# A state-space layer and an attention layer on one core: image 0's norm loaded and computed first, weight transforms behind it, one activation table for Ln and Exp

## The chip, the cores and the metric

The kernel runs on one core of a Trainium2 chip. The metric is device time in microseconds of one execution. Three runs of the kernel before took 3,012.99, 3,017.89 and 3,022.72 us; their median is 3,017.89 us.

A core has five engines that each take their instructions in order: TensorE (PE in the profile, with PEld for its weight loads), VectorE (DVE), ScalarE (ACT), GpSimd (POOL) and SyncE (SP), which here only issues transfers. They meet through semaphores. A DMA, too, is issued by one of the engines and counts up a semaphore when it lands. An engine whose next instruction waits holds everything that stands behind it, whether or not that could run.

## What is computed

The input x holds four images of 512 channels and 32 x 32 points, all in float32. Layer 0 is a selective state-space layer over the 1,024 points of an image, layer 1 attention between convolutions. Both have a group norm ahead of them and the input added behind them.

```python
# layer 0, features = _gn(x), one sequence of 1024 points per image
xn = (x - mu) / jnp.sqrt(var + 1e-05) * ln_w + ln_b
xz = xn @ W_in
xm, z = (xz[..., :d_inner], xz[..., d_inner:])       # d_inner = 1024
xs = silu(causal_conv4(xm) + conv_b)
proj = xs @ W_x
dt = jax.nn.softplus(proj[..., :dt_rank] @ W_dt + b_dt)
Bm, Cm = ...                                         # 16 states each
# for each point
dA = jnp.exp(dt_t[..., None] * A)
h = dA * h + (dt_t * x_t)[..., None] * B_t[:, None, :]
y = jnp.einsum('bds,bs->bd', h, C_t)
out = ((y + xs * D_param) * silu(z)) @ W_out
# layer 1, on _gn(x)
x_bottom = conv3x3(x, w_bottom); sp_map = softmax(center @ top)
out = conv3x3(x + sp_map @ x_bottom, w_out)
```

`_gn` is a norm over groups of 16 channels and all points.

## The kernel before

**Layer 0** (to about 1,975 us) handles four images. Of an image it makes the norm, eight channel blocks of 128 (`xs`, by `conv1`, or for image 0 by `conv1_half` in two halves of 512 points), the gates (`gates`), the small projections (`params`), and then for each pair of channel blocks e and each half h a stage of 16 units, one for each state. `delta` begins a stage: dt by a matmul, a bias and softplus on ACT, dt times x (`dtx`, L793) on POOL, its transposes on PE and their copies (`dtxt`) on ACT. A unit (`unit`) makes a decay by Exp on ACT, the input term on ACT and PE or on POOL, a scan on DVE, a product with C on POOL (or for four states on DVE), and adds into PSUM by PE. While one image's units run, the next image's norm and projections are worked in between.

**Order.** The instructions are not issued in the order of the code. Every helper calls `step(engine, time, fn, reads, writes, prio, ...)`, and `Plan.issue` then lays the steps out: at each turn it takes, for each engine, the steps that could begin soonest by its own estimates and of these the one with the lowest `prio`. A step can name an activation table ("ln", "exp", "silu", "softplus"); if it isn't the one that the plan has loaded last, the step counts as late and costs `LOAD`. Steps with `fill=True` may come early or late. Buffers come from rings with a fixed number of slots.

**Image 0's norm** (`norms`, called with prio -60) loads x in four chunks of 512 KB on SP (L409), takes statistics on DVE (L425, L426), averages over groups by two small matmuls (L433, L449) with `deviation` (L261 to L265) between them, takes Ln (L458) and Exp (L463) for the root, and builds weights `mw` for the mean over channels. Then for both halves of the points: mean by matmuls (`pmu`, L394), L518 on DVE, squares on ACT (L532, into the two buffers "res"), their mean by matmuls (`pvar`, L539), Ln of both halves (L550), Exp of both (L556), L565 on DVE and the affine step on ACT (L575). `conv1_half` follows with the weights `winc` (L598, ring of two), matmuls `pxm` (L394), a first tap on ACT (L671), three on DVE (L682) and Silu (L695).

**Weight pieces** (`transform`) turn the 3x3 weights of layer 1 into their transformed form: 18 of 32 pieces are made in layer 0, the rest in layer 1 on DVE. A piece loads three tiles of 192 KB on SP (L1164), scales on ACT (L1169, L1170), does twelve operations on POOL (L1177 to L1197) and writes twelve stores on SP (L1204). The first `t0` = 11 have prio -190, the others 60 units apart:

```python
transform(u, src, k % NPC, -190 if k < PRM['t0'] else PRM['tg'] * (k - PRM['t0']))
```

**Small loads.** The two bias rows `brow_b` and `brow_o` and the small constants (`lnw_sb`, `lnb_sb`, ..., `a_sb`, `wx_sb`) are loaded on ACT's queue. `a_sb` goes through Exp on ACT (L309) and a product with -1 on DVE (L310). All transfers of SP and ACT share eight completion semaphores, taken in turn as they are laid out, so an issue may have to wait for an earlier transfer that holds the same one.

**The border of the layers.** `first_image` norms image 0 of layer 1's input at the end of layer 0: `root` takes Ln (L255) and Exp (L256). The other three images do this in layer 1 (`norm`).

Of the kernel before, what the change touches and what calls it, by code (L numbers as in the profile page):

```python
# [27 lines left out]
GS = 16  # L28


PRM = dict(pg=0.53, kt=2, ke=1, ka=-0.68, fl=0, fi=4.6, m0=45.7, n0=50.77, nl=2.05, q0=65.56, qg=5.2, c0=61.67, cg=6.03, p0=112, e0=3.46, eg=4.75, g0=78.98, gg=9.04, o0=13.03, og=5.23, dl=10.28, t0=11, tg=60)


class Buf:
# [21 lines left out]
class Plan:  # L56
# [7 lines left out]
    def __init__(self, slots, in_order):  # L64
        self.slots, self.steps = dict(slots), []
        self.queues = {r: [] for r in in_order}

    def buf(self, ring, make):
# [35 lines left out]
    def issue(self):  # L104
        ready = {e: [s for s in self.steps if s.eng == e and not s.unmet] for e in self.ENGINES}
        clock = {e: 0.0 for e in self.ENGINES}
        free = {r: [0.0] * n for r, n in self.slots.items()}
        queues = {r: list(q) for r, q in self.queues.items()}
        table, dma, left = None, 0.0, len(self.steps)
        waiting = sorted((s for s in self.steps if not s.fill), key=lambda s: -s.prio)  # L110
        while left:
            while waiting and waiting[-1].done is not None:
                waiting.pop()
            last = waiting[-1].prio + self.AHEAD if waiting else 1e9
            best = None
            for e in self.ENGINES:
                urgent = min((s.prio for s in ready[e] if s.table in (None, table)), default=1e9)
                found = []
                for s in ready[e]:
                    if s.prio > last:  # L120
                        continue
                    t = max(clock[e], s.ready)
                    for b in s.takes:
                        turn = b.free or b.ring not in queues or queues[b.ring][0] is b
                        t = max(t, min(free[b.ring])) if free[b.ring] and turn else 1e9
                    if t >= 1e9:
                        continue
# [12 lines left out]
            for b in s.takes:  # L140
                free[b.ring].remove(min(free[b.ring]))
                if b.ring in queues and not b.free:
                    queues[b.ring].pop(0)
            s.fn()
            if late:
                t += self.LOAD
                table = s.table
            clock[s.eng] = t + s.us
            s.done = clock[s.eng] + self.LAG[s.eng]
            if s.kb:  # L150
                dma = max(dma, s.done) + s.kb / 300
                s.done = dma + 2.0
            for b in s.bufs:
                b.left -= 1
                if b.ring and not b.left:
                    free[b.ring].append(s.done + self.HOP)
                    if b.done:
                        b.done(b.tile)
            ready[s.eng].remove(s)
            for u in s.users:  # L160
                u.unmet -= 1
                other = u.eng != s.eng or s.kb
                u.ready = max(u.ready, s.done + self.HOP if other else clock[s.eng])
                if not u.unmet:
                    ready[u.eng].append(u)
            left -= 1
# [3 lines left out]
def mamba_then_pab_kernel(  # L170
# [29 lines left out]
    spool = ctx.enter_context(tc.tile_pool(name="spool", bufs=2))  # L200
    dram = ctx.enter_context(tc.tile_pool(name="dram", bufs=1, space=DRAM))

    gm_sb = cpool.tile([P, P], F32, tag="gmat", name="gm_sb")
    nc.sync.dma_start(gm_sb, gmat)
    ident = cpool.tile([P, P], F32, tag="ident", name="ident")
# [68 lines left out]
    with ExitStack() as l0:  # L274
# [4 lines left out]
        yp = l0.enter_context(tc.tile_pool(name="l0y", bufs=1, space=PSUM))  # L279
        up = l0.enter_context(tc.tile_pool(name="l0u", bufs=4, space=PSUM))  # L280

        NT = L // P
        NK = T // P
        QC = C // 4
# [47 lines left out]
        def dram_set(name, shape, n=B):  # L332
# [11 lines left out]
        }  # L344
        plan = Plan(
            {**slots, "mm": 2, "u": 4, "y0": 1, "y1": 1},
            ("xt", "u", "h", "cbc", "bb", "dbx", "sc"),
        )
        step = plan.step
        MM, TR = 0.88, 0.114  # L350
# [50 lines left out]
        def norms(b, prio, lag=0.0):  # L401

            t = xts[b] = buf("xt", [P, NCC, L], f"xt_{b}")
            src = x[b].rearrange("(c p) h w -> p c (h w)", p=P)
            xin = [buf(None, None, "") for c in range(NCC)]
            step("SP", 0.0, lambda: t(), [], [], prio, holds=[t])
            for c in range(NCC):
                step(
                    "SP", 0.3, lambda c=c: nc.sync.dma_start(t()[:, c, :], src[:, c, :]),  # L409
                    [], [xin[c]], prio, kb=512, holds=[t],  # L410
                )
            spl = {}
# [26 lines left out]
            def mid():  # L439
# [16 lines left out]
            step(  # L456
                "ACT", 0.2,
                lambda: nc.scalar.activation(spl["dev"], pv()[:, :NCC], AF.Ln, bias=eps),  # L458
                [pv], [stat], prio, "ln",
            )  # L460
            step(
                "ACT", 0.2,
# [37 lines left out]
            )  # L500
            by_half = [buf(None, None, "") for h in range(NH)]
            by_chunk = by_token(NCC)
            for h, hs in enumerate(halves):
                prio += lag
                pmu = group(f"pmu_{b}_{h}",
                    [
                        (
# [2 lines left out]
                        )  # L510
                        for c in range(NCC)
                    ],
                    prio, holds=[t],
                )
                for c in range(NCC):
                    step(
# [5 lines left out]
                        [pmu], [by_half[h]], prio, holds=[t],  # L522
                    )
            pvars = []
            for h, hs in enumerate(halves):
                prio += lag
                pvar = buf("mm", [P, T], f"pvar_{b}_{h}")
                for c in range(NCC):
                    sq = buf("res", [P, T], f"sq_{b}_{h}_{c}")
                    step(  # L530
                        "ACT", 0.61,
                        lambda c=c, hs=hs, sq=sq: nc.scalar.activation(  # L532
                            sq(), t()[:, c, hs], AF.Square, bias=spl["nb"][:, c : c + 1]
                        ),
                        [by_half[h], stat], [sq], prio, holds=[t],
                    )
                    step(
                        "PE", MM,
                        lambda c=c, sq=sq, pvar=pvar: nc.tensor.matmul(  # L539
                            pvar(), mean_w, sq(), start=(c == 0), stop=(c == NCC - 1)  # L540
                        ),
                        [sq], [pvar], prio,
                    )
                pvars.append(pvar)

            rs = [buf("res", [P, T], f"rs_{b}_{h}") for h in range(NH)]
            for r, pvar in zip(rs, pvars):
                step(
                    "ACT", 0.58,
                    lambda r=r, pvar=pvar: nc.scalar.activation(r(), pvar(), AF.Ln, bias=eps),  # L550
                    [pvar], [r], prio, "ln",
                )
            for r, pvar in zip(rs, pvars):
                step(
                    "ACT", 0.52,
                    lambda r=r, pvar=pvar: nc.scalar.activation(pvar(), r(), AF.Exp, scale=-0.5),  # L556
                    [r], [pvar], prio, "exp",
                )
            prio += lag

# [25 lines left out]
                    affine(c, slice(0, L), by_chunk[c])  # L586
            else:
                for h, hs in enumerate(halves):
                    prio += 0.01
                    for c in range(NCC):  # L590
                        scaled(c, h)
                        affine(c, hs, [by_chunk[c][h]])
# [174 lines left out]
        def delta(b, e, h, prio):  # L767
# [20 lines left out]
            dtx = buf("dtx", [P, 2, T], f"dtx_{name}")  # L788
            us = [xs[b, 2 * e + j] for j in range(2)]

            def times():
                for j in range(2):
                    nc.gpsimd.tensor_mul(dtx()[:, j], dt()[:, j], us[j]()[:, hs])  # L793

            step(
                "POOL", 2.46, times, [dt, *(xh[b, 2 * e + j][h] for j in range(2))], [dtx], prio,
                holds=us,
            )
            dtxt = buf("dtxt", [P, NK, 2, P], f"dtxt_{name}")
# [275 lines left out]
        def first_image(prio):  # L1075
# [61 lines left out]
                spl["rstd"] = spool.tile([P, NCC], F32, tag="grstd", name="grstd_image")  # L1137
                rsqrt(spl["rstd"], pv()[:, :NCC])

            step("ACT", 1.7, root, [pv], [stat], prio, "ln")  # L1140
            for c in range(NCC):
                step(
                    "DVE", 0.76,
# [567 lines left out]
```

## Time and profile before

| what | us |
|---|---|
| median of three runs (range) | 3,017.89 (3,012.99 to 3,022.72) |
| the profiled execution | 3,013.52 |
| its span, first to last instruction | 3,011.5 |
| busy: PE, DVE, ACT, POOL | 2,732.6, 2,324.8, 1,846.0, 2,054.5 |
| granted TensorE clock, mean | 0.972 |
| POOL's first product with C, stage e0 h0 of image 0 | 132.86 |
| the same of stage e0 h1 of image 0 | 237.75 |
| the same of stage e0 h0 of images 1, 2, 3 | 641.02, 1,104.72, 1,582.70 |

A page of the profile tells of one execution. A line of the timeline has the start, the length, the engine, the line of the kernel, the operation, output and inputs and a count; in brackets the time that the engine stood idle before it, and what ended it. A group has busy time and the mean time of one instruction in ns. The share of a stretch that an engine is busy says what sets the pace there, and the stretches of this kernel differ.

### The profile page before, as it was taken

The numbers are of one execution on the slowest core, as the hardware profiler recorded it, in microseconds if no ns is written. First come the engines' busy times: TensorE is split into PE (matmuls) and PEld (weight loads), VectorE is DVE, ScalarE is ACT, GpSimd is POOL, SyncE is SP. The second block draws the span as 40 slices with busy tenths as digits, with TensorE's granted clock in tenths as the row PEclk, the third lists the DMA queues.
The fourth block names the chain that finished last, engine by engine and source line by source line (L and its number), as shares of the span: only waits on it lengthen the run. The fifth ranks groups of instructions, "written<-read, shape, count | busy, mean of one in ns | idle before, by whom it ended". The sixth has DMA issues, their size and how long they took to land.

```text
span 3011.5 us, 35733 instructions
## 1 busy us (share of the span) xinstructions
PE 2732.6 (91%) x11512; PEld 1611.4 (54%) x11512; DVE 2324.8 (77%) x2787; ACT 1846.0 (61%) x3186; POOL 2054.5 (68%) x1239
## 2 busy tenths in 40 slices
PE   4789789999889999879899988889999999999998
PEld 2346566656666566656666666544444444444444
DVE  3468999989999889899888999986968565346264
ACT  4569999999799998789999898731210013021000
POOL 7999987899977799977799999942241442314122
PEclk9899999999999999989999999999999999999999
DMA  6765644577734467834557754648789896627497
GB/s 175 221 195 165 198 135 145 162 217 231 233 117 151 151 198 226 254 111 140 153 168 218 224 173 149 161 150 303 213 303 283 300 332 243 245 86 263 142 320 256
DMA packets 408945, 610.46 MB, mean 203 GB/s; under 512 B 46488, under 2 KB 245400, under 8 KB 384184
## 3 DMA queue, kind: packets, MB, share of 16 engines
q1 hardware_dynamic: 399952, 593.67, 62.0%
q10 hardware_dynamic: 8648, 14.26, 1.3%
q8 instruction: 92, 1.51, 0.2%
q14 instruction: 93, 0.76, 0.1%
q0 software_dynamic: 160, 0.26, 0.0%
HBM read 511.09 MB, written 96.99 MB: 202 GB/s over the span
## 4 chain that ended last, share of the span: by engine, by line
PE 39%; ACT 14%; DVE 14%; POOL 6%; issue 5%; DMA 4%; SPq 0%; DVEq 0%; POOLq 0%; ACTq 0%
PE m_o L1501 11%; PE m_b L1501 8%; PE pat L1553 4%; PE y L917 4%; ACT sc L844 3%; DVE da L884 3%; PE po L394 3%; POOL da L907 3%; PE pz L394 2%; ACT da L832 2%; ACT u L832 2%; PE u L870 2%; DVE u L884 2%; DVE dbx L884 2%; PE pp L730 1%
## 5 line engine op out<-in xcount | busy, mean ns | idle before, releaser
L907 POOL TENSOR_TENSOR da<-da,cbc 128x1024 f32<-128x1024 f32 x288 | 681.2, 2368 | 83.3 <-DVE da L884 58.3
L859 POOL TENSOR_TENSOR dbx<-dtx,bbc 128x1024 f32<-128x1024 f32 x224 | 529.5, 2371 | 35.7 <-PE y L917 18.7
L844 ACT ACTIVATE sc<-dtxt,bt_sb 128x256 f32<-128x256 f32 x1152 | 506.8, 497 | 48.6 <-PE u L870 48.1
L832 ACT ACTIVATE da<-dt,a_sb 128x512 f32<-128x512 f32 x576 | 398.6, 712 | 41.2 <-PE y L917 27.0
L917 PE MATMUL y<-ident,da 128*128 128x128 f32 x2304 | 318.4, 282 | 65.3 <-POOL da L907 59.4
L884 DVE TENSOR_TENSOR_SCAN da<-da,carry_sb,u 128x512 f32<-128x512 f32 x288 | 355.8, 1262 | 25.7 <-PE u L870 20.2
L870 PE MATMUL u<-ident,sc 128*128 128x128 f32 x2304 | 329.3, 279 | 35.1 <-DVE da L884 26.6
L917 PEld LDWEIGHTS y<-ident,da 128*128 128x128 f32 x2304 | 267.4, 145 | 166.1 <-POOL da L907 124.7
L884 DVE TENSOR_TENSOR_SCAN da<-da,u 128x512 f32<-128x512 f32 x288 | 338.4, 1202 | 18.6 <-PE u L870 16.7
L1501 PE MATMUL m_o<-uw_o,v_o 128*128 128x512 f32 x768 | 335.6, 596 | 7.4 <-DMA uw_o<-u_o 7.4
L1501 PE MATMUL m_b<-uw_b,v_b 128*128 128x512 f32 x768 | 333.7, 593 | 5.0 <-ACT e_b L1509 2.5
L870 PEld LDWEIGHTS u<-ident,sc 128*128 128x128 f32 x2304 | 268.5, 143 | 111.3 <-issue 36.4
L832 ACT ACTIVATE u<-dt,a_sb 128x512 f32<-128x512 f32 x448 | 296.0, 679 | 21.0 <-DVE dbx L884 7.4
L917 PE MATMUL y<-ident,dbx 128*128 128x128 f32 x1792 | 254.0, 282 | 29.3 <-POOL dbx L907 20.1
L394 PE MATMUL pxm<-xt,winc 128*128 128x345 f32 (+3 forms) x704 | 249.2, 498 | 27.6 <-DMA winc<-in_w_in_dram 17.1
L917 PEld LDWEIGHTS y<-ident,dbx 128*128 128x128 f32 x1792 | 212.5, 145 | 97.8 <-POOL dbx L907 36.9
L394 PE MATMUL pz<-xt,winc 128*128 128x512 f32 x512 | 243.2, 602 | 8.9 <-issue 3.1
L1501 PEld LDWEIGHTS m_b<-uw_b,v_b 128*128 128x128 f32 x768 | 144.9, 190 | 190.1 <-issue 180.8
L1501 PEld LDWEIGHTS m_o<-uw_o,v_o 128*128 128x128 f32 x768 | 144.8, 191 | 189.9 <-issue 177.3
L907 POOL TENSOR_TENSOR dbx<-dbx,cbc 128x1024 f32<-128x1024 f32 x96 | 227.1, 2365 | 7.1 <-DVE dbx L884 2.5
L1553 PE MATMUL pat<-y_b,st 128*128 128x512 f32 x512 | 223.3, 597 | 1.6 <-DVE rz L1562 1.5
L394 PEld LDWEIGHTS pxm<-xt,winc 128*128 128x128 f32 x704 | 132.1, 198 | 115.8 <-issue 43.5
(235 smaller groups left out, 4288.8 us busy)
## 6 DMA issues: line engine op xcount, KB each, us to landing
cbc<-bcd SPq DMA_DIRECT2D x512, 256.0 KB, 3.6
uw_b<-u_b SPq DMA_DIRECT2D x96, 1024.0 KB, 4.8
uw_o<-u_o SPq DMA_DIRECT2D x96, 1024.0 KB, 4.8
bbc<-bcd SPq DMA_DIRECT2D x224, 256.0 KB, 3.6
u_b<-work SPq DMA_DIRECT2D x192, 128.0 KB, 2.9
winc<-in_w_in_dram SPq DMA_DIRECT2D x72, 256.0 KB, 3.6
szd<-sz SPq DMA_DIRECT2D x32, 512.0 KB, 3.6
szl<-szd SPq DMA_DIRECT2D x32, 512.0 KB, 4.9
```

Source lines behind the costliest of these rows:

```text
L394: lambda k=k, lhs=lhs, rhs=rhs: nc.tensor.matmul(p()[:, at : at + cols], lhs(), rhs(), start=(k == 0), stop=(k == n - 1)),
L730: lambda d=d, hs=hs, pp=pp: nc.tensor.matmul(pp()[p0 : p0 + NP, :], wx_sb[:, d, :], xs[b, d]()[:, hs], start=(d == 0), stop=(d == NDC - 1),),
L832: nc.scalar.activation(t, dt()[:, j], AF.Exp, scale=a_sb[:, at : at + 1])
L844: nc.scalar.activation(sc()[:, k], dtxt()[:, k], AF.Copy, scale=bt[:, at, s : s + 1])
L859: lambda: nc.gpsimd.tensor_mul(hc(), dtx(), b_bc().to_broadcast([P, 2, T])),
L870: nc.tensor.transpose(u()[:, k * P : (k + 1) * P], sc()[:, k, j, :], ident)
L884: nc.vector.tensor_tensor_scan(ht, *((hc()[:, j], u()) if on_act else (u(), hc()[:, j])), carry_sb[:, j, s : s + 1] if h else 0.0, ALU.mul ...
L907: nc.gpsimd.tensor_mul(hc(), hc(), c_bc().to_broadcast([P, 2, T]))
L917: nc.tensor.matmul(y[j]()[:, k, :], hc()[:, j, k * P : (k + 1) * P], ident, start=(s == 0 and k == 0), stop=(s == NS - 1 and k == NK - 1), ...
L1501: nc.tensor.matmul(m[q], v[:, q, k, c, :], w[:, c, :], start=(c == 0), stop=(c == NCC - 1 and not extra),)
L1553: nc.tensor.matmul(pt, st[m][:, 2 * P * j + h : 2 * P * (j + 1) : 2], xb[m // 2][:, m % 2, :], start=(m == 0), stop=(m == NMC - 1),)
```

## The change

x of image 0 is loaded at the top of layer 0, by four instructions on SP that stand ahead of the plan; the steps that loaded it are empty for image 0 now. Two table names become one: "ln" steps are "exp" steps, and where the plan changes to "exp" it names the table set itself, one that has both functions; this is done once at the start, too. In `norms`, image 0's halves have their own places (`at_half`, half a unit apart), each with its squares, Ln, Exp, scaling and affine step; squares of image 0 go into buffers of the rings "dt" and "dtx" in place of "res". For the other images Ln and Exp of a half follow each other, and the places move by one `lag`. Places change for image 0's norm (-60 to -20), its `conv1_half` (-26 to -17), `params` (-24 to -16), the first `delta` (-23 to -15) and the pieces (-190 to -5, nine of them instead of eleven, the others 56 apart). The first `dtx` is made on VectorE.

```diff
-..., t0=11, tg=60)
+..., t0=9, tg=56)
@@ Plan.issue
-            s.fn()
             if late:
                 t += self.LOAD
                 table = s.table
+                if table == "exp":
+                    self.exp_set()
+            s.fn()
@@ the kernel
+    def exp_set():
+        nc.scalar.preload_act_table_set("natural_log_exp_and_others")
+
+    exp_set()
     gm_sb = cpool.tile([P, P], F32, tag="gmat", name="gm_sb")
...
+        first_x = xtp.tile([P, NCC, L], F32, tag="xt", name="xt_0", bufs=1)
+        for c in range(NCC):
+            nc.sync.dma_start(first_x[:, c, :], x[0, c * P : (c + 1) * P].rearrange("p h w -> p (h w)"))
@@ norms
+            if b == 0:
+                t.make = lambda: first_x
...
-                    "SP", 0.3, lambda c=c: nc.sync.dma_start(t()[:, c, :], src[:, c, :]),
+                    "SP", 0.3,
+                    lambda c=c: b and nc.sync.dma_start(t()[:, c, :], src[:, c, :]),
...
-                [pv], [stat], prio, "ln",
+                [pv], [stat], prio, "exp",
...
+            at_half = [prio + (lag * h if b else 0.5 * h) for h in range(NH)]
             for h, hs in enumerate(halves):
-                prio += lag
...
             for h, hs in enumerate(halves):
-                prio += lag
                 pvar = buf("mm", [P, T], f"pvar_{b}_{h}")
+                at = at_half[h] + (0 if b == 0 else NH * lag)
                 for c in range(NCC):
-                    sq = buf("res", [P, T], f"sq_{b}_{h}_{c}")
+                    if b:
+                        sq = buf("res", [P, T], f"sq_{b}_{h}_{c}")
+                        sqt = lambda sq=sq: sq()
+                    else:
+                        if c % 2 == 0:
+                            sq = buf(("dt", "dtx")[h], [P, 2, T], f"sq_{b}_{h}_{c}")
+                        sqt = lambda sq=sq, c=c: sq()[:, c % 2]
...
+            prio += 2 * NH * lag
-            for r, pvar in zip(rs, pvars):
+            for h, (r, pvar) in enumerate(zip(rs, pvars)):
+                at = prio if b else at_half[h]
                 step(
                     "ACT", 0.58,
                     lambda r=r, pvar=pvar: nc.scalar.activation(r(), pvar(), AF.Ln, bias=eps),
-                    [pvar], [r], prio, "ln",
-                )
-            for r, pvar in zip(rs, pvars):
+                    [pvar], [r], at, "exp",
+                )
...
-                    prio += 0.01
+                    prio = at_half[h]
@@ delta
+            on, eng, us_dtx = ("POOL", nc.gpsimd, 2.46) if b or e or h else ("DVE", nc.vector, 2.3)
...
@@ first_image
-            step("ACT", 1.7, root, [pv], [stat], prio, "ln")
+            step("ACT", 1.7, root, [pv], [stat], prio, "exp")
@@ the calls
-        norms(0, -60)
+        norms(0, -20)
         for d in range(NDC):
-            conv1_half(d, 0, -26 + 0.1 * d)
-        params(0, -24, (0,))
+            conv1_half(d, 0, -17 + 0.1 * d)
+        params(0, -16, (0,))
...
-            transform(u, src, k % NPC, -190 if k < PRM['t0'] else PRM['tg'] * (k - PRM['t0']))
+            transform(u, src, k % NPC, -5 if k < PRM['t0'] else PRM['tg'] * (k - PRM['t0']))
...
-                delta(b, e, h, (at + n * NS - PRM["dl"], -23, 9.6)[0 if b else {0: 1, 1: 2}.get(n, 0)])
+                delta(b, e, h, (at + n * NS - PRM["dl"], -15, 9.6)[0 if b else {0: 1, 1: 2}.get(n, 0)])
```

More of the change, by code (lines that the diff above doesn't have):

```diff
@@ L28 @@
 GS = 16
-PRM = dict(pg=0.53, kt=2, ke=1, ka=-0.68, fl=0, fi=4.6, m0=45.7, n0=50.77, nl=2.05, q0=65.56, qg=5.2, c0=61.67, cg=6.03, p0=112, e0=3.46, eg=4.75, g0=78.98, gg=9.04, o0=13.03, og=5.23, dl=10.28, t0=11, tg=60)
+PRM = dict(pg=0.53, kt=2, ke=1, ka=-0.68, fl=0, fi=4.6, m0=45.7, n0=50.77, nl=2.05, q0=65.56, qg=5.2, c0=61.67, cg=6.03, p0=112, e0=3.46, eg=4.75, g0=78.98, gg=9.04, o0=13.03, og=5.23, dl=10.28, t0=9, tg=56)
 class Buf:
@@ L62, with __init__ @@
     HOP, LOAD, SLACK, AHEAD = 0.05, 1.3, 0.07, 17.64
-    def __init__(self, slots, in_order):
-        self.slots, self.steps = dict(slots), []
+    def __init__(self, slots, in_order, exp_set):
+        self.slots, self.steps, self.exp_set = dict(slots), [], exp_set
         self.queues = {r: [] for r in in_order}
@@ L346, in mamba_then_pab_kernel @@
             {**slots, "mm": 2, "u": 4, "y0": 1, "y1": 1},
-            ("xt", "u", "h", "cbc", "bb", "dbx", "sc"),
+            ("xt", "u", "h", "cbc", "bb", "dbx", "sc"), exp_set,
         )
@@ L512, in norms @@
                     ],
-                    prio, holds=[t],
+                    at_half[h], holds=[t],
                 )
@@ L521, in norms @@
                         ),
-                        [pmu], [by_half[h]], prio, holds=[t],
+                        [pmu], [by_half[h]], at_half[h], holds=[t],
                     )
@@ L525, in norms @@
             for h, hs in enumerate(halves):
-                prio += lag
                 pvar = buf("mm", [P, T], f"pvar_{b}_{h}")
+                at = at_half[h] + (0 if b == 0 else NH * lag)
                 for c in range(NCC):
-                    sq = buf("res", [P, T], f"sq_{b}_{h}_{c}")
+                    if b:
[5 more added lines that the diff above has]
+                        sqt = lambda sq=sq, c=c: sq()[:, c % 2]
+                    sqh = buf(None, None, "")
                     step(
                         "ACT", 0.61,
-                        lambda c=c, hs=hs, sq=sq: nc.scalar.activation(
-                            sq(), t()[:, c, hs], AF.Square, bias=spl["nb"][:, c : c + 1]
+                        lambda c=c, hs=hs, sqt=sqt: nc.scalar.activation(
+                            sqt(), t()[:, c, hs], AF.Square, bias=spl["nb"][:, c : c + 1]
                         ),
-                        [by_half[h], stat], [sq], prio, holds=[t],
+                        [by_half[h], stat], [sqh], at, holds=[t, sq],
                     )
@@ L538, in norms @@
                         "PE", MM,
-                        lambda c=c, sq=sq, pvar=pvar: nc.tensor.matmul(
-                            pvar(), mean_w, sq(), start=(c == 0), stop=(c == NCC - 1)
+                        lambda c=c, sqt=sqt, pvar=pvar: nc.tensor.matmul(
+                            pvar(), mean_w, sqt(), start=(c == 0), stop=(c == NCC - 1)
                         ),
-                        [sq], [pvar], prio,
+                        [sqh], [pvar], at, holds=[sq],
                     )
                 pvars.append(pvar)
+            prio += 2 * NH * lag
             rs = [buf("res", [P, T], f"rs_{b}_{h}") for h in range(NH)]
-            for r, pvar in zip(rs, pvars):
+            for h, (r, pvar) in enumerate(zip(rs, pvars)):
+                at = prio if b else at_half[h]
                 step(
@@ L556, in norms @@
                     lambda r=r, pvar=pvar: nc.scalar.activation(pvar(), r(), AF.Exp, scale=-0.5),
-                    [r], [pvar], prio, "exp",
+                    [r], [pvar], at, "exp",
                 )
@@ L789, in delta @@
             us = [xs[b, 2 * e + j] for j in range(2)]
+            on, eng, us_dtx = ("POOL", nc.gpsimd, 2.46) if b or e or h else ("DVE", nc.vector, 2.3)
             def times():
                 for j in range(2):
-                    nc.gpsimd.tensor_mul(dtx()[:, j], dt()[:, j], us[j]()[:, hs])
+                    eng.tensor_mul(dtx()[:, j], dt()[:, j], us[j]()[:, hs])
             step(
-                "POOL", 2.46, times, [dt, *(xh[b, 2 * e + j][h] for j in range(2))], [dtx], prio,
+                on, us_dtx, times, [dt, *(xh[b, 2 * e + j][h] for j in range(2))], [dtx], prio,
                 holds=us,
```

## The prediction, made before the changed kernel was run

> **What bounds the kernel now.** I read the page's slices first, then busy time by stretch, then the timeline of the first 120 us, the waits of SP's queue, and last the order of instructions in both programs, which the planner decides.
>
> The slices show two halves: up to about 1,975 us (layer 0) four engines share the load, behind it (layer 1) TensorE alone is 94 to 100% busy. The change touches layer 0, and in layer 1 only table loads. By stretch (columns: stretch, length, busy us and instructions of PE, PEld, DVE, ACT, POOL, clock, DMA share, GB/s):
>
> ```profile
> 20.00:200.00 180.00, 134.34 (x348) 59.32 (x348) 76.72 (x118) 101.61 (x164) 161.33 (x159) 0.91 0.72 203
> 200.00:400.00 200.00, 166.54 (x930) 117.61 (x928) 181.86 (x211) 185.18 (x322) 191.66 (x111) 0.93 0.59 175
> 1480.00:1960.00 480.00, 427.91 (x2436) 294.46 (x2434) 446.24 (x493) 420.01 (x759) 456.49 (x268) 0.98 0.60 179
> ```
>
> The reader is to see the fifth pair, POOL: 161 of 180 us at the start, 192 of 200 behind it, 456 of 480 for the last image. In between it has slack (about 41 us idle in 400 to 620, 49 in 860 to 1,020, 53 in 1,300 to 1,480), where ACT or PE sets the pace. So POOL's work is dear at the start and in the last image.
>
> At the start POOL does weight pieces. One is 3 x 1.81 and 9 x 0.73 us, 12.3 with its gaps. They start at 19.85, 32.24, 45.7, 58.2, 75.7, 88.5, 100.9, 115.6, 136.5, 152.7, 169.6 and 184.6: twelve before the scans run at full pace, the last four between the first units. POOL is through with them at 197.15.
>
> The other early chain is image 0's norm:
>
> ```profile
> SPq L409 <- DMA lnw_sb<-in_ln_w_dram: 6.1, 1, 6.1
> SPq L409 <- DMA brow_b<-in_b_bottom_dram: 4.4, 1, 4.4
> ```
> ```profile
> 14.36 0.33 ACTq L297 DMA_DIRECT2D a_sb<-in_a_log_dram  x1
> ...
> 18.55 0.31 ACT L309 ACTIVATE a_sb<-a_sb 128x128 f32<-128x128 f32 x1 [6.14 <-DMA a_sb<-in_a_log_dram]
> 18.89 0.23 DVE L310 TENSOR_SCALAR a_sb<-a_sb 128x128 f32<-128x128 f32 x1 [3.27 <-ACT a_sb L309]
> 19.03 1.28 DVE L425 BATCH_NORM_STATS2 bs_l<-xt 128x6 f32<-128x512 f32 x2
> ...
> 22.89 1.28 ACT L463 ACT_TABLE_LOAD   x1
> 24.40 0.16 DVE L476 SCALAR_TENSOR_TENSOR gnb_l<-gmean_l,pv_l 128x4 f32<-128x4 f32 x1 [2.47 <-ACT pv_l L463]
> 35.24 5.36 DVE L518 SCALAR_TENSOR_TENSOR xt<-xt,grstd_l,pmu 128x512 f32<-128x512 f32 x8 [7.84 <-PE pmu L394]
> 46.61 1.28 ACT L550 ACT_TABLE_LOAD   x1
> 49.19 1.28 ACT L556 ACT_TABLE_LOAD   x1
> 55.17 1.08 SPq L598 DMA_DIRECT2D winc<-in_w_in_dram  x2
> 59.49 16.70 PE L394 MATMUL pxm<-xt,winc 128*128 128x512 f32 x32 [11.72 <-DMA winc<-in_w_in_dram]
> 65.93 0.69 ACT L671 ACTIVATE xs<-pxm,cw_sb 128x512 f32<-128x512 f32 x1 [7.45 <-PE pxm L394]
> 113.18 2.49 POOL L793 TENSOR_TENSOR dtx<-dt,xs 128x512 f32<-128x512 f32 x2
> ```
>
> Read in it: two of x's four loads waited on SP for tiny loads that hold the same completion semaphore; the last statistics stood behind a_sb on DVE; three table loads are in the chain; the first projection waited 11.7 us for a weight issued behind stores of pieces; dt, ready at 105.1, waited for POOL until 113.18.
>
> **The change, part by part** (times on before's clock).
>
> *x first.* Three of x's four loads now wait for nothing, the fourth for the first. But on DVE a_sb's product now stands in the middle of the deviation: behind that wait are its last two operations, PE's product for the variance, and ACT's Ln. And a_sb's load still waits for ln_b's semaphore (issued 8.41, 5.9 to landing, so 14.3): it issues near 14.4 and lands as now, 4.2 later, near 18.5. x may be through by 13 (2.4 MB from 2.2 us at the 200 to 315 GB/s of the slices); the group variance is then ready at 19.1 + 0.4 = 19.5 instead of 21.93. Gain **2.4**, not 7. (ACT's tiny loads crossed x traffic in before too; I leave their times.)
>
> *One table set.* The load at 22.89 goes: DVE starts at 19.5 + 0.68 + 0.3 + 0.2 = 20.7 instead of 24.40. Those at 46.61 and 49.19 go below. Here the Trainium skill (ScalarE: Activation LUTs, What ACT_TABLE_LOAD costs) prices a switch at 1.28 us plus a drain of 1.38. The rows have the 1.28, but no drain: Exp starts at 24.19, 0.02 after the load. By the row three loads are 3.8 us, by the page 8; I take the row.
>
> *Halves.* The first half's mean products now stand together: 8 passes, five at the cold spacing of 0.86 and three at 0.43, end 2.6 us before the old mixed order. DVE's L518 starts at 29.0 (before 35.24). Squares 29.8 to 32.7 (four of 0.72); their buffers are dt's and dtx's, so the stalls at two buffers (3.8 us on PE pvar) go. pvar at 34; Ln and Exp behind three squares of half 1, until 36.2; affine of half 0, behind a square and two piece scalings, 37.9 to 40.8; then Ln, Exp and affine of half 1 until 45.8. The winc weights are there since about 18, and PE stays warm (no 12 us gap, seven cold passes less, 3 us). First tap at 45.8 instead of 65.93: **20 us**.
>
> *Weight pieces behind it.* On SP their loads follow x and two winc loads, and the first winc waits for ln_w's semaphore (14.1) with all pieces behind it. They land near 19.5, so the first reaches POOL near 21.7, 1.9 later than now. Later winc loads stay between piece stores on SP: the third goes behind the second piece's (about 43.5, lands 47; before 65.92). Channels keep about 4 us each; proj at 74 to 76 (before 98.96).
>
> *First dt x on DVE.* Softplus ends near 82; DVE is free. By the nearest rows (L900 0.67, L960 0.69, one input in PSUM) two products cost 1.4. The Trainium skill (SBUF — State Buffer, Who interferes with whom) speaks against it: a VectorE instruction with two SBUF inputs and a GpSimd one that reads SBUF exclude each other, so each product may wait out a piece's 1.81, 5 in all. These rows show such a loss:
>
> ```profile
> L1383 DVE TENSOR_TENSOR v_b<-rr_b 128x1024 f32<-128x1024 f32 x12 | 32.4, 2704 | 0.0
> L1385 DVE TENSOR_TENSOR v_b<-rr_b 128x1024 f32<-128x1024 f32 x12 | 14.6, 1219 | 0.0
> ```
>
> The same shape, 1.5 us apart; that is 1.4 + 2 x 0.75 = 2.9, which I take, with 1.4 and 5 as ends. All of them are covered: PE turns dtx only behind the half-1 projections of channels 1 and 2, near 88.5, since channel 2's weight issues about 81.5. dtxt is copied at 91 instead of 116.9: **26**. If that cover went, 3 us more would be won. POOL loses 2.5.
>
> *POOL.* The order has ten pieces, not twelve, before full pace: 21.7 + 10 x 12.3 + 15 (the units between, without dtx) + idle. Idle is 18.8 in before's 20 to 200; the weight waits of 58 to 75 shrink, one wait of 3.4 for the scalings before piece 2 comes: I take 11. Sum 171 against 197.15: **26**, which PE and ACT reach as well. This is the head's gain; bounds 15 (the other chains need their old time) and 32.
>
> *Pieces put back.* By the order both programs have two pieces in each of images 0 to 2; after has two more in image 3, in its first and fourth stage. They cost 24.6 us where POOL has 23.5 idle of 480. Bounds: 3 (gaps take them) and 24.6. The stages take 47 to 54 us for 16 units, the pace of a POOL that never rests; I let the idle of the two stages take 7: **+17.5**.
>
> *Other table loads.* Behind the first stage layer 0 has 7 loads fewer, 9 us of ACT, around the norms of images 1 to 3, where POOL has slack and ACT is at 93 to 99%: half counts, **-4** (0 to -9). At the layers' border one of two (1985.74) lies beside a wait of DVE for PE: **-0.5**. Six in layer 1 lie beside a busy PE: 0. The norms of images 1 to 3 come one lag earlier, and the planner swaps neighbours here and there: 0, bounds ±6, since DVE's order is the same but for short swaps.
>
> Sum: -26 + 17.5 - 4 - 0.5 = **-13**. The profiled execution took 3,013.5 (span 3,011.5), so 3,000.5. The three runs' median is 4.4 above it (3,017.89, spread ±5), which gives 3,005; I put **3,001**, nearer the execution that the sum is made on.
>
> **Rivals.**
> 1. *The last image absorbs the pieces* (cost 3 to 6): its 23.5 us of POOL idle would have to be usable. For it: DVE is as full, so POOL need not be the bound. Against: idle there is in waits of 1 to 3 us, a piece's instructions come in order. -26 - 4.5 + 4 = -27: 2,987.
> 2. *The new wait eats the gain.* x is early, yet a_sb, channel 2's winc and the piece stores hold the chain, and stage 0 ends 15 to 18 earlier only: -16 + 17.5 - 4.5 = -3: 3,012.
> 3. *Slower: GpSimd in image 3.* Two pieces paid in full, 24.6, and a head whose gain is not over 10, because POOL's pieces still stall on ACT scalings that the planner put behind the norm. It decides from a head gain under some 15: -10 + 24.6 - 2 = +12.6: 3,028. For it: POOL 98 to 99% busy in 1,700 to 1,900. Against: two pieces out of a busy POOL must show.
>
> **How the numbers follow.** Likeliest case 0.45 (own range 2,993 to 3,010), absorbed 0.17, eaten 0.18, slower 0.20. What a measurement of this kernel tells from no change is about 0.3%, 9 us. Faster: 0.17 and four fifths of the likeliest, and little of the eaten, 0.55; same: the rest of these, 0.25; slower 0.20. The range leaves out the ends of rivals 1 and 3: 2,982 to 3,023.
>
> **What would show it.** First tap (ACT, xs<-pxm) near 46; Exp following Ln with no load; dtxt near 91; POOL's tenth piece done near 171; two L1199 groups behind 1,500 us, and stages 0 and 3 of image 3 some 9 us longer than 54 and 48. Wrong if the first full stage of scans (POOL's first product of stage 1, now 237.75) is not 15 to 32 earlier, or if image 3 doesn't lengthen.

## The result: slightly slower, and the profile after

The changed kernel took 3,023.59 us (median, 3,019.74 to 3,033.26); the kernel before, beside it, 3,017.28 (3,009.95 to 3,022.72). The ratio is 1.0025, with a 95% interval of 1.0017 to 1.0034. That is a loss of a quarter of a per cent where the prediction had a gain of half a per cent. Its profiled execution has a span of 3,021.4 us (before 3,011.5) at a mean clock of 0.971 (before 0.972).

The stretches first, with the columns of the prediction's rows (the five pairs are PE, PEld, DVE, ACT and POOL):

```profile
20.00:200.00 180.00, 150.52 (x425) 70.72 (x426) 95.92 (x133) 112.14 (x182) 153.71 (x144) 0.92 0.70 198
200.00:400.00 200.00, 164.90 (x949) 120.46 (x948) 188.44 (x221) 186.07 (x327) 191.06 (x111) 0.94 0.56 173
1480.00:1960.00 480.00, 416.97 (x2332) 287.81 (x2332) 426.02 (x467) 399.02 (x723) 448.48 (x270) 0.96 0.59 178
```

From 20 to 200 us PE does 16 us and DVE 19 us more than before, with 8 us less on POOL: the projections have come forward. In the last stretch the fifth pair, POOL, is lower than before (448 for 456) although the two new pieces are in it (before has one piece there, of image 2). This is a trap of fixed stretches: the kernel after comes into this one some 14 us further on and leaves it 10 us further back, so other units lie in it. The images have to be cut by their own units, as below.

Then image 0's norm on the timeline:

```profile
3.66 9.38 ACTq L307 DMA_DIRECT2D lnw_sb<-in_ln_w_dram  x1
...
15.71 0.44 ACTq L307 DMA_DIRECT2D a_sb<-in_a_log_dram  x1
...
19.53 0.31 ACT L319 ACTIVATE a_sb<-a_sb 128x128 f32<-128x128 f32 x1 [1.57 <-DMA a_sb<-in_a_log_dram]
...
19.88 0.23 DVE L320 TENSOR_SCALAR a_sb<-a_sb 128x128 f32<-128x128 f32 x1 [3.80 <-ACT a_sb L319]
...
21.06 0.26 ACT L471 ACTIVATE gdev_l<-pv_l,eps 128x4 f32<-128x4 f32 x1 [1.21 <-PE pv_l L462]
21.35 0.18 ACT L476 ACTIVATE pv_l<-gdev_l 128x4 f32<-128x4 f32 x1
...
23.69 1.81 POOL L1199 TENSOR_TENSOR work<-work 128x768 f32<-128x768 f32 x1 [16.10 <-ACT work L1191]
...
30.49 2.73 DVE L531 SCALAR_TENSOR_TENSOR xt<-xt,grstd_l,pmu 128x512 f32<-128x512 f32 x4 [5.92 <-PE pmu L404]
...
47.81 0.67 ACT L691 ACTIVATE xs<-pxm,cw_sb 128x512 f32<-128x512 f32 x1
```

Ln (21.06) and Exp (21.35) follow each other with no load between. The wait for a_sb on DVE is there, 3.80 us, as foreseen. The first tap comes at 47.81 (before 65.93), and dtxt, the copy that the first units need, at 95.75 (before 115.65). With x loaded first, other transfers wait on SP. Of its waits up to 130 us (us in all, times, longest):

```profile
SPq L1186 <- DMA u_b<-work: 9.7, 6, 5.4
SPq L618 <- DMA lnw_sb<-in_ln_w_dram: 8.5, 1, 8.5
```

Two things are read from it: winc waited 8.5 us for a load of ln_w, and loads of pieces waited for stores of pieces, 9.7 us in six waits.

So the head did come earlier. Where it went is seen when the execution is cut at the first product with C of three stages. Each column is the change of one interval's length against the kernel before, in us; the pieces of image 3 are the ones that `tg` = 56 put there.

| interval | before, us long | predicted | after |
|---|---|---|---|
| head: start to stage e1 h0 of image 0 | 290.6 | -26 | -25.8 |
| from there to the first unit of image 3 | 1,292.1 | -4 | +10.9 |
| image 3 to its last stage | 347.8 | +17.5 | +24.8 |
| last stage and layer 1 | 1,081.0 | -0.5 | 0.0 |
| sum | 3,011.5 | -13 | +9.9 |

### The profile page after: what moved, and what is told of

It is laid out like the page before. It is cut to its first block, busy times and chain, and to the rows that moved or that the text cites. A ratio compares the mean times of both kernels' runs of the same rounds, so it can differ in the third digit from the quotient of the medians.

```text
span 3021.4 us, 35682 instructions
## 1 busy us (share of the span) xinstructions
PE 2740.7 (91%) x11512; PEld 1622.2 (54%) x11512; DVE 2331.4 (77%) x2789; ACT 1824.4 (60%) x3168; POOL 2052.5 (68%) x1237
## 4 chain that ended last, share of the span: by engine, by line
PE 39%; DVE 14%; POOL 10%; ACT 9%; issue 6%; DMA 5%; SPq 1%; DVEq 0%; POOLq 0%; ACTq 0%
PE m_o L1523 11%; PE m_b L1523 8%; PE y L939 4%; POOL da L929 4%; PE pat L1575 4%; DVE da L906 3%; POOL dbx L881 3%; PE po L404 2%; PE u L892 2%; PE pz L404 2%; ACT sc L866 2%; PE pxm L404 2%; DVE u L906 2%; ACT da L854 2%; DVE dbx L906 1%
## 5 line engine op out<-in xcount | busy, mean ns | idle before, releaser
L854 ACT ACTIVATE da<-dt,a_sb 128x512 f32<-128x512 f32 x576 | 398.2, 713 | 45.5 <-PE y L939 33.3
L892 PE MATMUL u<-ident,sc 128*128 128x128 f32 x2304 | 336.2, 282 | 29.3 <-DVE da L906 20.4
L892 PEld LDWEIGHTS u<-ident,sc 128*128 128x128 f32 x2304 | 275.3, 146 | 100.0 <-issue 32.7
L404 PE MATMUL pz<-xt,winc 128*128 128x512 f32 x512 | 243.1, 603 | 12.4 <-DMA winc<-in_w_in_dram 5.7
```

Of the source, the lines that this page charges most:

```text
L404: lambda k=k, lhs=lhs, rhs=rhs: nc.tensor.matmul(p()[:, at : at + cols], lhs(), rhs(), start=(k == 0), stop=(k == n - 1)),
L854: nc.scalar.activation(t, dt()[:, j], AF.Exp, scale=a_sb[:, at : at + 1])
L892: nc.tensor.transpose(u()[:, k * P : (k + 1) * P], sc()[:, k, j, :], ident)
```

## The experiments

All kernels have the same arithmetic as before or after. "a_" and "s_" kernels start from the kernel after, "b_" kernels from the kernel before; in the lists each number is the place (`prio`) of one piece behind the first ones, where a unit counts 1, a stage 16 and an image 128.

### What the pieces cost in the last image, and in the others

a_img3out and a_slack differ from the kernel after in this line alone:

```diff
-transform(u, src, k % NPC, -5 if k < PRM['t0'] else PRM['tg'] * (k - PRM['t0']))
# a_img3out
+transform(u, src, k % NPC, -5 if k < PRM['t0'] else (0, 56, 112, 168, 224, 280, 320, 336, 352)[k - PRM['t0']])
# a_slack
+transform(u, src, k % NPC, -5 if k < PRM['t0'] else (0, 64, 80, 96, 192, 208, 224, 320, 336)[k - PRM['t0']])
```

> The kernel after, with its last two pieces taken out of the last image and made late in image 2 instead. Theory A (a piece costs its 12.3 us of GpSimd where GpSimd is full, and little where it has slack): the last image, from its first unit to the end, is back from 1453.6 to about 1429 us, image 2 grows by 3 to 8, total 3,000 to 3,006. Rival B (the last image is longer for another reason, the swapped order or a later start of its projections): the last image stays over 1445 us and the total over 3,015.

> The kernel after, with the last eight pieces in stages where GpSimd stood idle for 15 to 22 us each (from the fourth stage on of images 0, 1 and 2). Theory A: also the 5 to 8 us go that single pieces cost in the full stages of images 1 and 2; total 2,994 to 3,003, faster than before. Rival B (a piece costs about the same wherever it is): total as the kernel after, 3,020 to 3,026.

a_img3out: 3,000.55 us, ratio 0.9954 (0.9939 to 0.9969). Image 3 to the end measures 1,429.5 us, what theory A gave; image 2, which was to grow by 3 to 8 us, grew by 1.1. The first stage of image 3 by stretch, for the kernel before, after and a_img3out:

```profile
1582.70:1636.90 54.20, 48.73 (x278) 33.38 (x277) 45.97 (x55) 54.05 (x99) 51.02 (x33) 1.00 0.69 216
```
```profile
1567.80:1635.50 67.70, 55.26 (x283) 37.79 (x283) 48.07 (x55) 61.54 (x107) 65.05 (x47) 0.90 0.70 211
```
```profile
1567.90:1620.90 53.00, 48.88 (x282) 35.33 (x280) 45.72 (x54) 52.49 (x95) 50.90 (x34) 0.97 0.68 216
```

The fifth pair again: with the piece POOL does 65.05 us in 67.70, without it 50.90 in 53.00. Its idle time stays at 2 to 3 us, so nothing of the piece's 12.3 us went into a gap; the stage grew by all of it (and by two products of dt and x that lie in it besides).

a_slack: 2,978.44 us, ratio 0.9876 (0.9857 to 0.9894), below the expected range. The price of the places in images 0 to 2 had been put too low even after the result was known. Against a_img3out four pieces lie elsewhere (out of image 0's e3 h0, image 1's e1 h0 and image 2's e0 h1 and e2 h1, into image 0's e2 h0 and e2 h1 and image 1's e1 h1 and e2 h0), and that gave 22 us by the medians, not 5 to 8.

s_one puts a single one of them back, from prio 208 to 168:

```diff
-(0, 64, 80, 96, 192, 208, 224, 320, 336)
+(0, 64, 80, 96, 168, 192, 224, 320, 336)
```

> a_slack with a single piece moved: out of image 1's stage e2 h0 (20 us of GpSimd idle before) into its stage e1 h0 (1 us idle). Theory A (the price is the idle time that the stage's GpSimd lacks): stage e1 h0 grows from 49.5 to 57 to 60 us, stage e2 h0 keeps its 68 to 69; total 8 to 11 us over a_slack, 2,986 to 2,990. Rival B (places within a mid image don't matter): total 2,975 to 2,981.

It took 2,985.97 us, ratio 0.9916 (0.9901 to 0.9930): over a_slack 7.5 us by the medians, just short of theory A's 8 to 11, and 0.4% by the ratios. Stage e1 h0 of image 1 in a_slack, and then its stage e2 h0:

```profile
719.30:768.80 49.50, 46.43 (x264) 32.05 (x263) 46.16 (x55) 40.07 (x76) 48.54 (x32) 1.00 0.78 253
831.20:899.10 67.90, 58.36 (x300) 41.10 (x300) 64.98 (x86) 62.78 (x102) 56.03 (x42) 0.95 0.49 144
```

and stage e1 h0 in s_one:

```profile
718.60:777.80 59.20, 54.67 (x284) 35.39 (x283) 47.13 (x55) 41.03 (x77) 57.85 (x44) 1.00 0.80 248
```

In the first line POOL is busy 48.54 of 49.50 us; the piece makes the stage 59.20, 9.7 longer, and not 12.3, as one of the units' own POOL products (`dbx`, 2.4 us) less lies in it, six for seven. In the second line, stage e2 h0 has a piece in it, and POOL still idles 12 of 67.90 us; without it, in s_one, that stage measures 68.2. Part of the piece's room came from other work: with the piece five `dbx` products lie in e2 h0, without it eight, and with it the next stage is 3.1 longer. From e2 h0 to the end of image 1 the four stages take 248.7 us with the piece and 248.3 without. **The same twelve instructions cost 9.7 us in one stage and next to nothing in the other.** The kernel after has a piece in just this stage e1 h0 (59.4 us).

### What brought the head forward

```diff
# a_t11: the kernel after with the piece parameters of before
-..., t0=9, tg=56)
+..., t0=11, tg=60)
# b_t9: the kernel before with those of after
-..., t0=11, tg=60)
+..., t0=9, tg=56)
```

> The kernel after, with the piece parameters of before (eleven pieces first, the rest 60 apart). Theory A (the head is bound by GpSimd's pieces, so the early norm and the single table set bring little by themselves): the first unit of the second stage (stage e0 h1 of image 0) is back near 237, the last image at 1429; total 3,012 to 3,019, no different from before. Rival C (the 20 us of the head come from the earlier norm): second stage stays near 218 to 222, total 2,996 to 3,002.

> The kernel before, with only the piece parameters of after (nine pieces first, the rest 56 apart). Theory A (the head is bound by GpSimd): two pieces fewer give 15 to 24 us at the head, the last image loses 25; total 3,013 to 3,024. Rival C (the head is bound by the norm and the chain behind it): nothing is won at the head, the last image still loses 25; total 3,035 to 3,043.

a_t11: 3,013.31 us, ratio 0.9994 (0.9985 to 1.0003). b_t9: 3,038.09 us, ratio 1.0073 (1.0056 to 1.0090). The start of stage e1 h0 of image 0, in a square of the two parts:

| | eleven first | nine first |
|---|---|---|
| norm of before | 290.6 | 280.7 (b_t9) |
| norm of after | 290.0 (a_t11) | 264.8 (after) |

The early norm alone gives 0.6 us, two pieces fewer alone 9.9, both 25.8. Neither theory was right by itself (a_t11's total is theory A's, but the second stage came at 242.77, later than the 237 that it gave): two chains of nearly the same length end at the first stages. Stage e0 h0 of image 0 in a_t11 shows the one that is left when the norm is early:

```profile
110.20:242.80 132.60, 86.82 (x333) 50.14 (x332) 60.39 (x74) 75.86 (x122) 118.91 (x105) 0.83 0.62 181
```

POOL's 118.91 of 132.60 us is far above every other engine. b_t9's total met rival C's number but not its reason: it won 9.9 at the head and lost 9.4 again before image 3, with the pieces at the places of the kernel after and the same long stages (59.3 us in e1 h0 of image 1, 54.8 in e0 h1 of image 2); image 3 cost 23.5.

### The small parts

```diff
# b_slack: the kernel before, nine pieces first and the others at the places of a_slack
+transform(u, src, k % NPC, -190 if k < PRM['t0'] else (0, 64, 80, 96, 192, 208, 224, 320, 336)[k - PRM['t0']])
# s_ln: a_slack without exp_set, Ln in the set "ln" again
-                if table == "exp":
-                    self.exp_set()
-                [pv], [stat], prio, "exp",
+                [pv], [stat], prio, "ln",
-                    [pvar], [r], at, "exp",
+                    [pvar], [r], at, "ln",
-            step("ACT", 1.7, root, [pv], [stat], prio, "exp")
+            step("ACT", 1.7, root, [pv], [stat], prio, "ln")
# s_pool: a_slack with the first dt x on GpSimd
-            on, eng, us_dtx = ("POOL", nc.gpsimd, 2.46) if b or e or h else ("DVE", nc.vector, 2.3)
+            on, eng, us_dtx = ("POOL", nc.gpsimd, 2.46)
```

> The kernel before, with nothing changed but the places of the pieces: nine first, and the other nine where a_slack has them. Theory A (places alone: nothing lost in the full stages of images 1 and 2, nothing in the last image, 10 us won at the head as in b_t9): 2,988 to 2,996, and the start of image 0's second pair of channels (stage e1 h0) near 281. Rival C (the early norm is not needed, the places bring all): 2,976 to 2,982. Rival D (the places bring nothing without the early norm): 3,008 or more.

> a_slack with Ln and Exp in separate table sets again, Ln and Exp of each half still in turn. The head has GpSimd as its bound, so the loads there are hidden there (0 to 3 us at stage e1 h0); behind it they cost ACT about 4 us by the prediction's term: total 2,980 to 2,986. Rival (loads in the norms hold whole chains): 2,990 or more. None if they are all hidden: 2,977 to 2,979.

> a_slack with the first dt x product back on GpSimd (2.5 us of it). If the head is bound by GpSimd: stage e1 h0 of image 0 2 to 4 us later, total 2,980 to 2,983. Rival (dt's wait for GpSimd held the first stage, 8 us in the kernel before): 5 us or more. If it is hidden: no change from 2,978.

b_slack: 2,999.08 us, ratio 0.9950 (0.9937 to 0.9962), a miss of all three: it won the 10 us at the head, lost 10.9 in the rest of image 0 (where a_slack with the same places loses 1.5; the cause stays open), and 12.7 came back until image 3. Against a_slack's 0.9876 the norm part of the change is worth some 0.7% once the pieces lie well.

s_ln: 2,980.01 us, ratio 0.9885 (0.9871 to 0.9898), with 185 table loads for 171. s_pool: 2,981.61 us, ratio 0.9890 (0.9876 to 0.9905). Both intervals hold a_slack's ratio, so neither part can be told from nothing. By the profiles s_ln is 3.1 us behind a_slack between the head and image 3; in s_pool the head is 1.2 later. In s_ln the copy dtxt comes 4.3 us later than in a_slack (100.75 for 96.41), and the head is none the later for it (263.8 for 265.1). So with nine pieces first the norm's chain seems to have a few us to spare; this is not shown cleanly, as the planner's order differs too (the tenth piece is done at 170.6 for 182.2).

### How far pieces can leave the head

```diff
# s_t6: a_slack, six first
+t0=6 ... (0, 64, 80, 96, 112, 192, 208, 224, 240, 320, 336, 352)[k - PRM['t0']]
# s_t4: four first
+t0=4 ... (0, 64, 72, 80, 96, 112, 192, 200, 208, 224, 240, 320, 336, 352)[k - PRM['t0']]
# s6_brow (s_t6) and s4_brow (s_t4): bias rows loaded behind wdt_sb, scaled late
-        nc.scalar.activation(t, t, AF.Copy, scale=-12.0)
+        for t in brow:
+            step("ACT", 0.63, lambda t=t: nc.scalar.activation(t, t, AF.Copy, scale=-12.0), [], [], 200)
```

> a_slack with six pieces first instead of nine, the three others in the fourth slack stage of each image. Theory A (the head is still bound by GpSimd, and slack stages take a piece for 1 to 3 us): stage e1 h0 of image 0 starts at 230 to 245 instead of 265, total 2,955 to 2,970. Rival (with nine pieces the norm's chain, ACT and TensorE bind the head as closely as GpSimd): stage e1 h0 at 258 or later, total 2,974 to 2,984.

> s_t6 with two more pieces taken from the head (four first) and put into the slack stages of images 0 and 1. If GpSimd still binds the head: stage e1 h0 of image 0 8 to 12 us earlier than s_t6's 249.9, total 2,950 to 2,957. If the norm's chain, ACT and TensorE bind it now (stage e0 h0 had 18.5 us of GpSimd idle in s_t6): within 3 us of 249.9, total 2,960 to 2,968.

> s_t6 with the two bias rows loaded behind the small constants, so that a_sb and ln_w don't stand behind them on ACT's queue. The wait of 3.9 us for a_sb in the deviation goes, Ln of the norm starts at 17 to 18 instead of 21.6, the first tap (first xs from pxm) comes at 43 to 45 instead of 48. If this chain binds the head with six pieces first: total 2,956 to 2,960. If not: 2,960 to 2,965, with the 4 us lost again before stage e1 h0.

> Both together: bias rows behind the small constants, four pieces first. If the chain of the norm is what is late once pieces are out of the way: stage e1 h0 of image 0 at 244 to 247 and the total 2,952 to 2,958. If the head is bound elsewhere (ACT with units and projections): the total is that of s_t4 within 3 us.

| kernel | head | to image 3 | image 3 | rest | median, us | ratio (95% interval) |
|---|---|---|---|---|---|---|
| after | -25.8 | +10.9 | +24.8 | 0.0 | 3,023.59 | 1.0025 (1.0017 to 1.0034) |
| a_t11 | -0.6 | -3.6 | +0.9 | +4.3 | 3,013.31 | 0.9994 (0.9985 to 1.0003) |
| b_t9 | -9.9 | +9.4 | +23.5 | +1.5 | 3,038.09 | 1.0073 (1.0056 to 1.0090) |
| a_img3out | -27.9 | +13.1 | -1.2 | +1.8 | 3,000.55 | 0.9954 (0.9939 to 0.9969) |
| a_slack | -25.5 | -9.2 | -0.8 | +1.6 | 2,978.44 | 0.9876 (0.9857 to 0.9894) |
| s_one | -27.5 | +1.9 | -0.7 | -1.1 | 2,985.97 | 0.9916 (0.9901 to 0.9930) |
| s_t6 | -40.7 | -7.0 | -1.1 | +3.6 | 2,962.34 | 0.9827 (0.9810 to 0.9844) |
| s_t4 | -47.2 | +1.6 | -1.0 | +1.3 | 2,969.08 | 0.9852 (0.9837 to 0.9867) |
| s6_brow | -47.8 | -7.8 | -1.0 | +0.7 | 2,962.35 | 0.9830 (0.9817 to 0.9843) |
| s4_brow | -50.4 | +1.8 | 0.0 | +2.2 | 2,965.01 | 0.9839 (0.9826 to 0.9853) |

(The four columns are intervals of one profiled execution each, against the kernel before. Kernels that are the same up to stage e1 h0, as a_slack and s_one, differ there by 2 us.)

**s_t6 beats both kernels**, by 1.7% against the kernel before. Three pieces less at the head (36.9 us of POOL) gave 15 us, the next two 6.5: the bound has passed to other work. The expectations had more from it: s_t6's stage e1 h0 starts at 249.9, above the range of theory A, and the totals of s_t4 and s4_brow lie in neither of their two ranges. Stage e0 h0 of image 0 in s_t6 and in s_t4:

```profile
110.30:196.30 86.00, 76.22 (x318) 42.44 (x317) 66.63 (x75) 64.40 (x103) 67.45 (x48) 0.92 0.54 153
```
```profile
106.80:189.70 82.90, 74.50 (x323) 42.33 (x322) 66.85 (x81) 71.46 (x109) 51.19 (x34) 0.98 0.42 127
```

POOL has 18.6 and 31.7 us idle there, and TensorE is the fullest engine. s_t4 gives back between the head and image 3 what it won. All of it goes in the rest of image 0, which is 8.6 us longer than in s_t6; half of that is stage e2 h0, which has two pieces (68.0 for 63.6). Image 1, where e2 h0 has two as well, is no longer as a whole (465.4 for 465.6). s6_brow did to its chain what was expected of it:

```profile
16.92 0.26 ACT L469 ACTIVATE gdev_l<-pv_l,eps 128x4 f32<-128x4 f32 x1 [3.66 <-PE pv_l L460]
...
43.73 0.67 ACT L689 ACTIVATE xs<-pxm,cw_sb 128x512 f32<-128x512 f32 x1
```

Ln starts 4.7 us earlier than in s_t6 and the first tap 4.6 (48.28 there), and in the profiles the head gains 7. The times do not show it: ratios of 0.9830 and 0.9827, with runs of s_t6 spread from 2,957.73 to 2,971.05. Whether it is worth anything stays open.

## Why the prediction was wrong

**The step that failed is "by the order both programs have two pieces in each of images 0 to 2".** From the equal number it took an equal cost, none, and looked at places only for the two pieces of image 3. But `tg` = 56 for 60 also moved five of the six others: from image 0's e3 h1, image 1's e3 h0 and image 2's e1 h0 and e3 h0 to image 0's e3 h0, image 1's e2 h1 and image 2's e0 h1 and e2 h0, and within e1 h0 of image 1 from the ninth unit, where most of the piece ran over into the next stage, to the third. With the new norm and the old places (a_t11) the interval between the head and image 3 is 3.6 us shorter than before; with the new places (after) it is 10.9 longer. The term that was put at 0 is +14.5: 5.8, 3.6 and 5.2 us in images 0, 1 and 2. The dearest stages are e1 h0 of image 1 (+7.0 against a_t11) and e0 h1 of image 2 (+6.5), where POOL is full; s_one shows the first by itself. The second, in after and then in a_t11:

```profile
1148.25:1203.16 54.91, 50.61 (x263) 33.53 (x262) 47.82 (x50) 45.14 (x81) 53.92 (x34) 0.97 0.83 263
```
```profile
1163.80:1212.19 48.39, 47.13 (x264) 31.68 (x263) 47.14 (x49) 42.73 (x81) 44.60 (x22) 1.00 0.73 220
```

POOL idles 3.8 of 48.39 us without the piece and 1.0 of 54.91 with it. Not all of the 14.5 is traced: stages that lost a piece gave back less (3.0 us in e1 h0 of image 2, 3.6 in e3 h0 of image 1), and image 0's e1 h1, which has a piece in both kernels, is 2.9 longer, with one `dbx` product more in it.

**The second step, mis-sized: "I let the idle of the two stages take 7".** The two pieces of image 3 cost 24.8, in b_t9 23.5; removed, the image is as long as before. That is the full price of two pieces (24.6), the upper bound of the sum. POOL's idle time in such a stage is 1 to 3 us and remains whatever else it does: in the first stage 3.2 us before, 2.6 with the piece, 2.1 in a_img3out. The first stage grew by 13.5 us where some 9 had been named; the second piece ran over, with 2.9 in the fourth stage, 6.2 in the next and 3.1 behind it. Rival 3 had this place right. It went with a head that gains 10, and the head gained 25.8; the other 14.5 came from a place that no rival named. That its total, 3,028, lies near the 3,023.59 is luck: its misses of 15.8 us at the head and 12.9 behind it nearly cancel.

**The head's 26 was right, in part by luck.** At stage e0 h1, where the prediction had set its sign, the gain is 20.0 us (217.75 for 237.75); at e1 h0 it is 25.8. The milestones: variance matmul at 20.43 where the deviation was foreseen ready at 19.5; DVE's first scaling (L531) at 30.49 for 29.0; first tap 47.8 for 45.8; dtxt 95.75 for 91. The norm's steps were each 1 to 2 us late. The tenth piece was done at 181.9, not 171, which is 15 us before the twelfth of the kernel before (197.15) and not 26: POOL idled 26.3 us between 20 and 200, where 18.8 had been read before and 11 were taken. The group of a piece's first operation in that stretch (busy, mean ns; idle before it, some of it ahead of the stretch, and what ended it) has it:

```profile
L1199 POOL TENSOR_TENSOR work<-work 128x768 f32<-128x768 f32 x10 | 18.1, 1813 | 28.3 <-ACT work L1191 25.1 <-DMA u_b<-work 3.0
```

Of the row's 28.3 us, 12.4 lie ahead of 20. Of the 26.3 behind it, 12.7 are waits for the scalings on ACT, the stall that rival 3 had named, 7.3 are waits for stores of earlier pieces, and the rest is short gaps. What this took away came back in part in stage e0 h1 of image 0, shorter by 5.8 us (47.1 for 52.9), which no step foresaw: seven of the units' `dbx` products (2.4 us each) lie in it for nine. a_t11, with the same norm, has it too (47.3). The clause "which PE and ACT reach as well" carried more than it was given: the square above shows that each part needs the other, and that fewer pieces alone give 9.9, less than the lower bound of 15.

**Table loads.** No drain behind the load: right, 0.02 us between the load (86.30) and what follows (87.60), as in the row. "Other table loads -4": a_t11 gives -3.6, s_ln 3.1 the other way; the last interval alone, mostly layer 1, differs by 4.3 between after and a_t11, so the size is plausible and not shown.

**dt x on DVE.** Two products took 1.81 us, below the 2.9 taken and above the 1.4 of no interference. As said, it was covered.

**Slips on which nothing rests.** POOL's idle time from 860 to 1,020 is 45.5 us, not 49, and it is busy 97% from 1,700 to 1,900, not 98 to 99. By their own terms rival 2 comes to 3,010.5 and rival 3 to 3,026, not 3,012 and 3,028.

## What to carry over

Work that is "filled in" has no price of its own: where its engine sets the pace it costs its whole duration (24.8 us for two pieces in image 3) or most of it, and where that engine idles 12 to 20 us of a stage next to nothing: in s_one 9.7 us against 0.4 for the same instructions. When a change shifts a spacing parameter, list every item that it moves with the idle time of the stage that it lands in, before and after, instead of counting items by image. And where two chains end together, neither edit shows its worth alone; try them as a square.

## What the runs showed of the hardware

A VectorE instruction with two inputs in SBUF and an operation of GpSimd shut each other out, and even one element pays. In the kernel after, a product of one element per partition ran beside a piece's operation:

```profile
85.94 1.80 DVE L707 SCALAR_TENSOR_TENSOR xs<-tails,cw_sb,xs 128x1 f32<-128x1 f32 x1
...
88.32 0.21 DVE L707 SCALAR_TENSOR_TENSOR xs<-tails,cw_sb,xs 128x2 f32<-128x2 f32 x1
...
89.24 1.81 DVE L815 TENSOR_TENSOR dtx<-dt,xs 128x512 f32<-128x512 f32 x2
```
```profile
85.93 1.80 POOL L1209 TENSOR_TENSOR work<-work 128x768 f32<-128x768 f32 x1
87.68 0.73 POOL L1217 TENSOR_TENSOR work<-work 128x256 f32<-128x256 f32 x1
88.50 0.73 POOL L1218 TENSOR_TENSOR work<-work 128x256 f32<-128x256 f32 x1
89.31 1.19 POOL L1219 TENSOR_TENSOR work<-work 128x256 f32<-128x256 f32 x1
90.46 1.17 POOL L1217 TENSOR_TENSOR work<-work 128x256 f32<-128x256 f32 x1
```

L707 takes 0.20 to 0.21 us where GpSimd is idle (at 96.55 and 109.06) or has some 0.1 us of an operation left, as at 88.32, and 1.80 where it lies over L1209, to the hundredth of a microsecond; and while the products with dt run (89.24), the two operations of POOL beside them take 1.19 and 1.17 for 0.73. The Trainium skill (SBUF — State Buffer, Who interferes with whom) calls the shared port an exclusive lock, and these rows agree; the loser is whichever comes second, on either engine.

An issue on ACT's queue can take long for a tiny load: ln_w's took 9.38 us (5.17 before) behind two bias rows that are read element by element, and with those rows moved behind the small loads (s6_brow) it took 0.40, and a_sb, six loads later, was issued at 6.11 instead of 15.78 (s_t6).
